# A Mamba loop issued in the order of its text, with two head phases per step and decays four steps ahead

## The chip, the cores and the metric

One core of one Trainium2 chip runs the kernel. The time is the device time of one launch in microseconds (us). The kernel before takes 10208.33 us (median of 4 runs, 10189.17 to 10220.28). "PEclk" or "granted clock" is the share of full speed that the clock throttle let TensorE have. In the listings PE is TensorE, DVE is VectorE, ACT is ScalarE and POOL is GpSimd. L654 is line 654 of that kernel's file, so one operation has different line numbers in different kernels.

## The reference, cut to what matters

The whole is an attention block, a Mamba layer along the image, a two-way Mamba along rows and then along columns, and a small filter. The change touches only the Mamba parts:

```python
# one Mamba: x [channel 128, time], state 16 per channel
xc = silu(conv4(x) + b);  z = gate projection of the same input
dt, B, C = split(x_proj(xc));  dt = softplus(dt_proj(dt) + dt_b)
h  = exp(dt * A) * h + dt * B * xc          # for every state: the scan
y  = (sum over states of h * C) + xc * D
out = out_proj(y * silu(z))
```

## The kernel before

The sequence is cut into units of 768 columns. There are 120: 24 in layer 1 and two passes of 48 in layer 2 (rows, then columns). A unit has a head (convolution, gate, Silu, softplus, B, C), 16 steps (a decay `da`, an input `u_s`, a scan, a product with C), four pairs of gathers, and a tail. Heads are generators: each `yield` is a place where the loop does a step of the recurrence first.

```python
def head(self, u):
    raw = self.work("raw", 2 * CH)                  # two buffers
    for j in range(2):
        p = self.convolved(u, u.c0 + j * HALF)      # four products, one PSUM tile "m"
        yield
        nc.scalar.activation(u.xc[:, halves[j]], p, AF.Identity, bias=w.conv_b)
    ...                                             # two gate products, copied to raw
    self.k.tc.keep_in_program_order(nc.scalar.activation(raw, raw, AF.Silu))
    self.table = nc.scalar.preload_act_table_set("natural_log_exp_and_others")
    ...
    for j in range(2):
        p = self.mm(w.step, u.xc[:, halves[j]])     # dt_proj, a half at a time, tile "m"
        yield
        nc.scalar.activation(e[:, halves[j]], p, AF.Abs, bias=w.dt_b)
        nc.scalar.activation(u.dt[:, halves[j]], p, AF.Relu, bias=w.dt_b)
    nc.scalar.activation(e, e, AF.Exp, scale=-1.0)
    nc.scalar.activation(log, e, AF.Ln, bias=1.0)
    ...
    nc.vector.tensor_scalar(kept, e, 1.0, 1.0, ALU.add, ALU.subtract)
    ...                                             # GpSimd: e, log, dt, u, memset of dt

def gather(self, u, step):                          # y_ssm: four small products
    ...
    if q == 3:                                      # twice per unit
        nc.vector.scalar_tensor_tensor(yv, u.xc[:, cols], u.w.Dp, u.py[:, :HALF], ALU.mult, ALU.add)
        nc.gpsimd.tensor_mul(u.y[:, cols], yv, u.gate[:, cols])

def run(self, units):
    ...
    for n, (u, s) in enumerate(steps):
        if s == 1:
            other = chain(self.head(units[i + 1]), units[i - 1].tail(units[i - 1]))   # shortened
        if s == self.STEPS - 2:
            for _ in other:
                pass
        self.spread(at(n + 1), at(n + 2))           # u_s of the next step, dt_s of the one after
        self.scan(u, s)                             # VectorE: multiply u_s by B, scan
        next(other, None)
        if s % 2 == 0 and n >= 2:
            self.gather(*steps[n - 1])
```

The order in which each engine gets these instructions is not the order of this text: a scheduler of the framework arranges them. In PSUM, `dt_s` has one buffer, `u_s` two, the gather one, and all other products share the one buffer "m". The trace has two records for each product of the text, so the four products of a gather are its x8.

## Time and profile before

| before (profiled run, span 10211.9 us) | value |
|---|---|
| granted clock, whole span | 0.858 |
| VectorE busy | 7503.5 us (73%) |
| TensorE busy | 8743.6 us (86%) |
| layer 1, from one unit's `kept` to the next | 59.5 us |
| layer 2, the same, first and last pass | 56.6 and 55.9 us |

The number after the second bar of a group is idle time of the engine right before these instructions, and the arrow names what ended it. Three more groups of the kernel before, from the view of groups with different shapes kept apart, are needed later. They are VectorE's other operations that depend on TensorE or ScalarE:

```profile
L676 DVE SCALAR_TENSOR_TENSOR yv<-raw,cols,y_ssm 128x384 f32<-128x384 f32 x240 | 141.4, 589 | 10.3 <-PE y_ssm L665 10.3
L578 DVE TENSOR_SCALAR kept<-e 128x768 f32<-128x768 f32 x120 | 82.9, 691 | 81.5 <-ACT e L569 81.4
L869 DVE SCALAR_TENSOR_TENSOR xa<-lin,cols,xa 64x384 f32<-64x384 f32 x96 | 75.6, 788 | 58.9 <-PE lin L867 58.9
```

The reader is to see that all three are small: before the change, VectorE's idle time in the Mamba part is the 1146 us ahead of the multiply, some 0.1 us ahead of each scan, and little else.

### The profile page before, as it was taken

What the parts mean: (1) busy time and instruction counts of PE and PEld (TensorE: products, weight loads), DVE (VectorE), ACT (ScalarE), POOL (GpSimd) and SP (SyncE); (2) the same over time, 40 slices, a digit from 0 to 9 for tenths busy, and PEclk for the clock granted to TensorE, in tenths of its full rate; (3) what the DMA queues carried; (4) which work ended last, traced back from release to release, by engine and by line L of the source; (5) the groups of instructions that cost most, each with busy time, mean ns of one, the idle gap of its engine ahead of it and who ended that gap; (6) DMA issues with size and microseconds to landing.
All of it is one profiled execution on the core that took longest, in us unless ns stands there. A gap on an engine that the chain in (4) does not pass through costs nothing.

```text
span 10211.9 us, 100390 instructions
## 1 busy us (share of the span) xinstructions
PE 8743.6 (86%) x38998; PEld 2948.9 (29%) x38998; DVE 7503.5 (73%) x6112; ACT 4291.8 (42%) x5082; POOL 4701.9 (46%) x3186
## 2 busy tenths in 40 slices
PE   9999999999868888868888888888688888888884
PEld 3333333333222222222222222222222222222221
DVE  4666646666658777767787777777778777787778
ACT  3444434444334334434444444444344444444442
POOL 0000000000036666636666666666367666676663
PEclk9999989999977777768888888888688888898887
DMA  0000000000000000000000000000000000000000
GB/s 24 1 1 1 1 1 1 1 1 1 1 0 1 1 1 1 1 0 1 1 1 1 1 1 1 1 1 1 0 1 1 1 1 1 1 1 1 1 1 19
DMA packets 2220, 17.25 MB, mean 2 GB/s; under 512 B 196, under 2 KB 324, under 8 KB 1096
## 3 DMA queue, kind: packets, MB, share of 16 engines
q1 hardware_dynamic: 1440, 9.44, 0.2%
q8 instruction: 307, 5.03, 0.2%
q14 instruction: 177, 1.45, 0.0%
q10 hardware_dynamic: 296, 1.33, 0.0%
HBM read 6.05 MB, written 4.72 MB: 1 GB/s over the span
## 4 chain that ended last, share of the span: by engine, by line
PE 27%; DVE 24%; POOL 15%; issue 5%; ACT 2%; DVEq 0%; POOLq 0%; ACTq 0%
DVE h L652 13%; PE u_s L622 7%; POOL hc L654 7%; DVE u_s L642 7%; PE y_ssm L665 6%; PE conv L536 4%; PE mm L513 4%; POOL e L579 2%; POOL log L580 2%; POOL dt L584 2%; PE dt_s L622 1%; PE conv L530 1%; DVE h L648 1%; POOL yg L677 1%; PE lin L863 1%
## 5 line engine op out<-in xcount | busy, mean ns | idle before, releaser
L654 POOL TENSOR_TENSOR hc<-h,C 128x768 f32<-128x768 f32 x1920 | 3484.0, 1819 | 1746.0 <-DVE h L652 1551.5
L652 DVE TENSOR_TENSOR_SCAN h<-da,u_s 128x768 f32<-128x768 f32 x1536 | 2693.8, 1754 | 199.5 <-DVE u_s L642 4.8
L633 ACT ACTIVATE da<-dt_s 128x768 f32<-128x768 f32 x1920 | 1554.2, 809 | 2936.6 <-PE dt_s L622 2914.2
L642 DVE TENSOR_TENSOR u_s<-u_s,B 128x768 f32<-128x768 f32 x1920 | 1825.6, 951 | 1146.0 <-PE dt_s L622 1059.0
L622 PE MATMUL u_s<-u,spread 32*128 32x384 f32 x7680 | 2221.5, 629 | 429.3 <-DVE h L652 325.5
L622 PE MATMUL dt_s<-dt,decay 32*128 32x384 f32 x7680 | 2119.3, 630 | 8.7 <-ACT da L633 3.5
L267 DVE TENSOR_TENSOR acc_e<-acc_e,e 128x1536 f32<-128x1536 f32 x792 | 1390.0, 1755 | 763.4 <-ACT e L211 724.7
L665 PE MATMUL y_ssm<-hc,gather 128*32 128x384 f32 x7680 | 1433.9, 598 | 457.9 <-POOL hc L654 456.6
L211 ACT ACTIVATE e<-f_exp 128x1536 f32<-128x1536 f32 x864 | 1207.0, 1449 | 1218.4 <-PE f_exp L201 1218.4
L622 PEld LDWEIGHTS u_s<-u,spread 32*128 32x128 f32 x7680 | 775.5, 217 | 1871.8 <-DVE h L652 805.9
L240 POOL TENSOR_TENSOR xa<-xa,t_att 64x512 f32<-64x512 f32 x36 | 45.3, 1259 | 2725.1 <-ACT t_att L238 2725.1
L218 PE MATMUL y_att<-e,xb 128*64 128x512 f32 x5184 | 1242.5, 601 | 0.0
L201 PE MATMUL f_exp<-theta,phi 64*128 64x512 f32 x5184 | 1235.7, 608 | 0.6 <-ACT e L211 0.6
L536 PE MATMUL conv<-xb,taps 64*128 64x384 f32 (+3 forms) x1536 | 694.2, 604 | 118.2 <-ACT raw L550 117.5
L648 DVE TENSOR_TENSOR_SCAN h<-da,state,u_s 128x384 f32<-128x384 f32 x768 | 737.4, 1000 | 48.4 <-DVE u_s L642 1.0
L622 PEld LDWEIGHTS dt_s<-dt,decay 32*128 32x128 f32 x7680 | 692.4, 217 | 186.7 <-ACT da L633 126.7
L201 PEld LDWEIGHTS f_exp<-theta,phi 64*128 64x128 f32 x5184 | 468.8, 187 | 756.7 <-issue 463.4
L665 PEld LDWEIGHTS y_ssm<-hc,gather 128*32 128x32 f32 x7680 | 232.0, 116 | 1429.7 <-POOL hc L654 854.4
L218 PEld LDWEIGHTS y_att<-e,xb 128*64 128x64 f32 x5184 | 341.3, 136 | 830.7 <-issue 830.1
L513 PE MATMUL mm<-raw,bc 128*128 128x384 f32 x960 | 519.2, 627 | 27.7 <-ACT dt L568 23.0
L550 ACT ACTIVATE raw<-conv,cols 128x384 f32<-128x384 f32 x240 | 139.6, 582 | 909.6 <-PE conv L536 415.1
L536 PEld LDWEIGHTS conv<-xb,taps 64*128 64x128 f32 x1536 | 332.7, 227 | 457.1 <-ACT raw L550 180.4
(147 smaller groups left out, 6005.7 us busy)
## 6 DMA issues: line engine op xcount, KB each, us to landing
xa<-in_x SPq DMA_DIRECT2D x6, 768.0 KB, 10.1
out<-xb SPq DMA_DIRECT2D x4, 1152.0 KB, 4.4
mats<-in_mats ACTq DMA_DIRECT2D x1, 1218.0 KB, 7.8
cols<-in_cols ACTq DMA_DIRECT2D x1, 71.5 KB, 9.5
dtw<-in_dtw ACTq DMA_DIRECT2D x1, 10.0 KB
```

The source lines that it names most:

```text
L201: nc.tensor.matmul(fs[j // 3][:, bass.ts(j % 3, NB)], lhsT=phi[at, bass.ts(m // 2, P)], rhs=theta[at, bass.ts(i, NB)], start=True, stop=True,)
L211: nc.scalar.activation(e, f, AF.Exp)
L218: nc.tensor.matmul(y[rows_of(m % 2)], lhsT=g[:, m, :], rhs=es[j // 3][:, bass.ts(j % 3, NB)], start=m < 2, stop=m >= KEYS - 2,)
L267: nc.vector.tensor_add(acc, acc, e)
L513: self.nc.tensor.matmul(p[:, :HALF], lhsT=lhsT, rhs=rhs, start=True, stop=True)
L536: self.nc.tensor.matmul(p3[:, :, o], lhsT=lhsT, rhs=x3[:, :, i], **flags)
L622: self.nc.tensor.matmul(self.side((u.pu if what == 0 else u.pda)[step], j), lhsT=(self.t.spread if what == 0 else u.w.decay)[rows, q], rhs ...
L633: self.nc.scalar.activation(da, u.pda[step][:, NB - HALF : NB + HALF], AF.Exp)
L642: nc.vector.tensor_mul(two(bx), two(bx), each(u.B))
L652: nc.vector.tensor_tensor_scan(h[:, way], da[:, way], bx[:, way], 0.0, ALU.mult, ALU.add)
L654: nc.gpsimd.tensor_mul(two(hc), two(h), each(u.C))
L665: nc.tensor.matmul(u.py[32 * r : 32 * r + 32, :HALF], lhsT=self.t.gather[:, q], rhs=u.hc[s][:, j * HALF : (j + 1) * HALF], start=q == 0, s ...
```

## The change

The intent is to take the order of the Mamba loop out of the scheduler's hands and write it down. The `with tc.manual_schedule()` block issues instructions as the text has them. The head of the next unit starts one whole unit ahead (`LEAD = 16`) and moves by two phases per step: one between the spreads and the exp of a decay, one behind that exp. Decays run four steps ahead (`AHEAD = 4`) in six buffers, `raw` has three, `hc` (the product with C) six in place of five, and the gathers come two steps later. `dt_p`, the step product, is now one 768-wide tile in the single buffer of `dt_s`, so that Abs and Relu are one instruction each.

```diff
-        raw = self.work("raw", 2 * CH)
+        raw = self.work("raw", 2 * CH, bufs=3)
...
-        for j in range(2):
-            p = self.mm(w.step, u.xc[:, halves[j]])
-            yield
-            nc.scalar.activation(e[:, halves[j]], p, AF.Abs, bias=w.dt_b)
-            nc.scalar.activation(u.dt[:, halves[j]], p, AF.Relu, bias=w.dt_b)
+        p = self.ps_da.tile([P, 2 * NB], FP, tag="p", name="dt_p")
+        for j in range(2):
+            nc.tensor.matmul(self.side(p, j), lhsT=w.step, rhs=u.xc[:, halves[j]], start=True, stop=True)
+        v = p[:, NB - HALF : NB + HALF]
...
+        nc.scalar.activation(e, v, AF.Abs, bias=w.dt_b)
+        nc.scalar.activation(u.dt, v, AF.Relu, bias=w.dt_b)
+        yield
...                          # more yields: about two per step of the recurrence
-            self.spread(at(n + 1), at(n + 2))
+            self.inputs(at(n + 1))
+            later = at(n + self.AHEAD)
+            p = self.decays(later)
+            next(head, None)
+            next(tail, None)
+            self.decay(later, p)
+            if s == self.STEPS - self.LEAD and i + 1 < len(units):
+                head = self.head(units[i + 1])
+            if s == self.STEPS - 2 and i:
+                tail = units[i - 1].tail(units[i - 1])
+            next(head, None)
+            next(tail, None)
             self.scan(u, s)
-            next(other, None)
-            if s % 2 == 0 and n >= 2:
-                self.gather(*steps[n - 1])
+            if s % 2 == 0 and n >= 4:
+                self.gather(*steps[n - 3])
...
-        m.run(units)
+        with tc.manual_schedule():
+            m.run(units)
```

## The prediction

> **What bounds the kernel now.** I read the page's 40 slices first, then the costliest groups, then the timeline of single units in the second half. The slices show two regimes: until slice 11 the attention, which the diff does not touch, and from about 2940 us the five Mamba passes.
>
> ```profile
> PE   9999999999868888868888888888688888888884
> ...
> DVE  4666646666658777767787777777778777787778
> ...
> PEclk9999989999977777768888888888688888898887
> ```
>
> In the Mamba part no engine is full: TensorE reads 8, VectorE 7 to 8. The groups say what VectorE waits for:
>
> ```profile
> L654 POOL TENSOR_TENSOR hc<-h,C 128x768 f32<-128x768 f32 x1920 | 3484.0, 1819 | 1746.0 <-DVE h L652 1551.5
> L652 DVE TENSOR_TENSOR_SCAN h<-da,u_s 128x768 f32<-128x768 f32 x1536 | 2693.8, 1754 | 199.5 <-DVE u_s L642 4.8
> L633 ACT ACTIVATE da<-dt_s 128x768 f32<-128x768 f32 x1920 | 1554.2, 809 | 2936.6 <-PE dt_s L622 2914.2
> L642 DVE TENSOR_TENSOR u_s<-u_s,B 128x768 f32<-128x768 f32 x1920 | 1825.6, 951 | 1146.0 <-PE dt_s L622 1059.0
> ```
>
> A step is one multiply and one scan on VectorE, 1.07 + 1.67 = 2.74 us from start to start. A layer-2 unit has 16 steps (43.84), the `kept` operation (0.45), two `yv` (1.0) and its share of the tail (0.85): 46.1 us of VectorE. The timeline has 48 such units from 4547.69 to 7271.57, so 56.7 us each: 10.6 us of holes. Layer 1 (step 2.90, 49.0 us of work) takes 1431.5/24 = 59.6 us, also 10.6 us of holes. The 1146 us of idle time before the multiply, over 120 units, is nearly all of it. The timeline shows two big holes per unit. The first, where one unit follows another:
>
> ```profile
> 6014.47 1.75 DVE L652 TENSOR_TENSOR_SCAN h<-da,u_s 128x768 f32<-128x768 f32 x1
> ...
> 6017.39 1.81 POOL L586 TENSOR_TENSOR u<-dt,raw 128x768 f32<-128x768 f32 x1
> ...
> 6019.49 0.97 DVE L642 TENSOR_TENSOR u_s<-u_s,B 128x768 f32<-128x768 f32 x1 [3.26 <-PE dt_s L622]
> ```
>
> The head's GpSimd chain (e, log, dt, u) ends too late, and the new unit's spreads wait for it. The second, four to six steps later:
>
> ```profile
> 6037.97 1.00 POOL L677 TENSOR_TENSOR yg<-yv,raw 128x384 f32<-128x384 f32 x1
> 6039.00 0.58 ACT L550 ACTIVATE raw<-conv,cols 128x384 f32<-128x384 f32 x1 [3.80 <-POOL yg L677]
> ...
> 6039.63 4.43 PE L536 MATMUL conv<-xb,taps 64*128 64x384 f32 x8 [1.75 <-ACT raw L550]
> ...
> 6047.14 0.97 DVE L642 TENSOR_TENSOR u_s<-u_s,B 128x768 f32<-128x768 f32 x1 [5.08 <-PE dt_s L622]
> ```
>
> ScalarE may not write the next `raw` until GpSimd has used the old gate (two buffers); TensorE waits, then runs the second convolution in 4.43 us, where the first, at 6034.23, took 2.80.
>
> **What the Trainium skill says.** "TensorE: Matmul & The Clock Gate", Part 1, has the clock halve after an idle window of about 3.4 us and return after a busy one. The trace agrees: between 4600 and 7200 us I sorted TensorE's gaps by the rate of the first products after them. Of gaps under 1.25 us 1 of 125 led to half rate, of 1.25 to 2.25 us 49 of 98, of 3.25 to 3.75 us 37 of 37. "ScalarE: Activation LUTs", section "What ACT_TABLE_LOAD costs", gives about 1283 ns a load; the trace has two of 1.28 around each Silu:
>
> ```profile
> 6050.40 1.28 ACT L556 ACT_TABLE_LOAD   x1
> 6051.70 1.48 ACT L556 ACTIVATE raw<-raw 128x1536 f32<-128x1536 f32 x1
> ...
> 6053.20 1.28 ACT L557 ACT_TABLE_LOAD   x1
> ...
> 6054.49 0.81 ACT L633 ACTIVATE da<-dt_s 128x768 f32<-128x768 f32 x1
> ```
>
> so 4.09 us in which ScalarE does no exp. "PSUM — Partial Sum Buffer", section "Engine vs sequencer instructions", says that ScalarE, VectorE and GpSimd queues are strict FIFO and matmuls start in program order. That decides this change: before, the order was a scheduler's; afterwards it is the text's, and an instruction that waits holds back everything behind it.
>
> **The change, part by part.** Work is nearly unchanged: one 768-wide Abs and Relu replace two 384-wide each, and decays lead by four steps instead of two. What it removes: with three `raw` buffers and the head from step 0 on, the second hole's cause is gone (5 us); with u and dt ready at step 12, so is the first hole's (3 us). Both were worth about 8 of the 10.6.
>
> What it adds I get by walking one layer-2 unit in text order. Durations from the timeline: the four spreads of a step run together in 0.93 us (half rate 1.65); spread to exp 1.02; product 0.84 to the next, convolution half 2.73 (half rate 4.36), gather 0.78 (half rate 1.44). T(n) is the start of multiply n; the spreads of step n start at T(n)+0.14, because u_s(n+1) needs scan n−1's buffer, so 1.6 us of TensorE delay is free.
> - Steps 0 to 2, two convolutions in front of u_s(2) and u_s(3): the third multiply comes 0.95 us late. Where a real tail lies there (every second unit) its `lin` products (about 3 us each) stall VectorE 2.4 us instead. Mean 1.7.
> - Step 4, Silu: exp(8) ends at T4+2.3 (TensorE is 0.35 late there), loads and Silu until T6+0.9, exp(9) T6+1.7. `dt_p` shares the single dt_s buffer, so it starts only then: 1.7 us of product, Abs and Relu 1.75, dt_s(10) 0.95, exp(10) 0.85, Exp of e 0.85: T6+7.8. `kept` stands in VectorE's queue in front of multiply 7, which was due at T6+2.74. Loss 5.1. TensorE idles over 3 us ahead of `dt_p`, so mostly the clock halves: 1.6 to 2 us more.
> - Step 12: the memset of dt stands on GpSimd behind hc(10), dt, hc(11) and u, so it ends at T13+1.9. dt_s(16) waits for it in TensorE's queue, then the gather, then u_s(14): multiply 14 is 1.95 late, and since TensorE idled 3.6 us, at half rate 3.8. Layer 1 has no memset and loses nothing here.
>
> Layer 2 at full clock: 1.7 + 5.1 + 1.95 = 8.75, thus 54.9 us per unit; with the half rate about 12.5, thus 58.6. Layer 1: 0.5 + 4.4 + 0.3 gives 54.2, with the half rate 56.4. Against 56.7 and 59.6:
> - full clock: 96 × (−1.8) + 24 × (−5.4) = −303 us, 9910;
> - half rate in each such gap: 96 × 1.9 + 24 × (−3.2) = +106 us, 10320.
> The first decays, now four one after another, cost three passes about 3 us each, 10 in all.
>
> **The rivals.** (a) VectorE becomes the bound: text order with four decays in hand hides everything; units take 46 to 48 us and the time is about 9100 to 9300. For it: VectorE steps already run at 2.74 without gaps for ten steps on end, and the constants look tuned. Against it: `kept` and the shared `dt_p` buffer in the walk above. (b) The new waits only replace the old ones: the sum with the half rate, 10300. For it: 37 of 37 long gaps halve the clock. Against: a stall also gives the other engines time to catch up, and I may have put a phase wrong by one step. (c) TensorE becomes the bound: 16 × 0.93 + 8 × 0.78 + 5.5 + 8 × 0.84 + 3 = 36 us per unit at full clock, far under 46; only a clock at half throughout would do it, some 65 us and 11000. The granted 0.85 speaks against that.
>
> **Range and chances.** The walk spans 9910 to 10320, with its middle near 10120; I take 10110, a little under, since a change of this kind is usually made to win and my error in reading an order is more likely to have invented a stall than to have missed a hole. Range 9650 to 10430. Faster by over 2% means under 10008: 0.39. Within 2%: 0.43. Slower: 0.18.
>
> **What would show it.** In the changed profile the idle time before L642's multiply because of dt_s should fall from 1059 to under 400 us; the idle time before `kept` should rise from under 60 us to 300 to 700, ended by ACT e; ScalarE's Abs should wait on `dt_p`; a wait of dt_s for the memset should appear on TensorE in layer 2 only; the 3.8 us ScalarE wait on yg should be gone. Layer 1 should gain more per unit than layer 2. If `kept` shows no idle time, the walk is wrong and rival (a) holds. If the mean matmul stays at 600 ns or more, the half rate is as I feared.

## The result and the profile after

The changed kernel takes 10840.35 us (median of 4, 10818.72 to 10861.24) against 10208.33 us. The ratio is 1.0621, with a 95% interval from 1.0593 to 1.0649: slower by 6.2%. Ratios here are the mean time of one kernel's fast runs over that of the other's of the same rounds, so they differ a little from the ratio of the medians. The predicted 10110 us and the range up to 10430 were wrong.

The slices of the changed kernel's page, 40 over a span of 10859.5 us:

```profile
PE   9999999999587787677777777777777777777874
...
PEclk9999989999778777577877787776677777777776
```

Against before, most of TensorE's 8s are now 7s, and in the second half the granted clock is mostly 7, in places 6, where it was mostly 8. The view of windows shows the last pass (48 units), first of the kernel before, then of the changed one. The columns are the window, then its length, the busy time of PE, PEld (weight loads), DVE, ACT and POOL with the number of instructions, the granted clock, and the DMA share and rate.

```profile
7408.00:10096.00 2688.00, 2272.95 (x10994) 758.33 (x10992) 2133.68 (x1725) 1151.93 (x1566) 1823.56 (x1098) 0.85 0.00 1
```

```profile
7674.00:10743.00 3069.00, 2402.70 (x10972) 808.54 (x10968) 2126.91 (x1724) 1146.48 (x1470) 1814.82 (x1098) 0.73 0.00 1
```

VectorE does the same work (2134 and 2127 us) in 381 us more. So the loss is idle time of VectorE, not work. Measured from one `kept` to the next, a layer-2 unit takes 62.7 us in the first pass and 64.0 in the last (before 56.6 and 55.9). A layer-1 unit takes 57.9 (before 59.5): layer 1 did gain.

VectorE's groups of the changed kernel, shapes kept apart, show where the idle time is (`kept` now lies in the buffer of `u`, hence its name `u<-e`):

```profile
L664 DVE TENSOR_TENSOR_SCAN h<-da,u_s 128x768 f32<-128x768 f32 x1536 | 2693.8, 1754 | 197.0 <-DVE u_s L654 5.3 <-POOL yg L689 1.0 <-ACT da L646 1.0
L654 DVE TENSOR_TENSOR u_s<-u_s,B 128x768 f32<-128x768 f32 x1920 | 1820.2, 948 | 635.3 <-PE dt_s L629 581.2 <-PE u_s L629 50.9
L688 DVE SCALAR_TENSOR_TENSOR yv<-raw,cols,y_ssm 128x384 f32<-128x384 f32 x240 | 144.3, 601 | 340.1 <-PE y_ssm L677 340.1
L896 DVE SCALAR_TENSOR_TENSOR xa<-lin,cols,xa 64x384 f32<-64x384 f32 x96 | 75.8, 790 | 120.1 <-PE lin L894 120.1
L584 DVE TENSOR_SCALAR u<-e 128x768 f32<-128x768 f32 x120 | 67.2, 560 | 842.7 <-ACT e L578 842.7
```

The multiply lost 511 us of idle time, as intended. `kept` gained 761, `yv` 330, the tail's `lin` 61. The balance is +641 us, and the spans differ by 648: the account closes.

Two groups of TensorE name what it waits for:

```profile
L629 PE MATMUL dt_s<-dt,decay 32*128 32x384 f32 x7680 | 2264.5, 673 | 398.3 <-POOL dt L608 332.1 <-ACT dt L571 37.3 <-ACT da L646 21.7
L565 PE MATMUL dt_p<-raw,step 128*128 128x384 f32 x480 | 346.0, 876 | 336.6 <-ACT da L646 326.5
```

The decays of the next unit wait 332 us for the memset of dt (L608), and `dt_p` waits 327 us for an exp of ScalarE, because it shares the single buffer of `dt_s`. The same in time, from the timeline of one layer-2 unit (start, length, engine, instruction, and in brackets the engine's idle time before it):

```profile
5995.75 0.81 ACT L646 ACTIVATE da<-dt_s 128x768 f32<-128x768 f32 x1
5996.61 2.36 PE L565 MATMUL dt_p<-raw,step 128*128 128x384 f32 x4 [2.58 <-ACT da L646]
...
5999.87 0.89 ACT L571 ACTIVATE dt<-dt_p,cols 128x768 f32<-128x768 f32 x1
6000.81 1.65 PE L629 MATMUL dt_s<-dt,decay 32*128 32x384 f32 x4 [0.26 <-ACT dt L571]
...
6004.08 0.56 DVE L584 TENSOR_SCALAR u<-e 128x768 f32<-128x768 f32 x1 [6.19 <-ACT e L578]
...
6018.84 1.65 PE L629 MATMUL u_s<-u,spread 32*128 32x384 f32 x4 [2.34 <-DVE h L664]
...
6023.77 0.11 POOL L608 MEMSET dt<- 128x8 f32 x1
...
6023.94 1.65 PE L629 MATMUL dt_s<-dt,decay 32*128 32x384 f32 x4 [3.45 <-POOL dt L608]
6025.52 1.51 PE L677 MATMUL y_ssm<-hc,gather 128*32 128x384 f32 x8
...
6028.66 0.97 DVE L654 TENSOR_TENSOR u_s<-u_s,B 128x768 f32<-128x768 f32 x1 [4.39 <-PE dt_s L629]
```

The first hole: a table load and Silu hold up an exp, that exp holds the buffer that `dt_p` needs, the exp of `e` comes after Abs, Relu and one more decay, and `kept` stands in VectorE's queue for it, 6.19 us, ahead of a multiply whose inputs were there. The second: dt_s for the next unit waits 3.45 us for the memset, and then the gather and the next u_s still stand in front of the multiply. The four records of one `dt_s` take 0.91 us at full clock (from 6035.22 on in this unit) and 1.65 here: TensorE ran at half rate behind both gaps. The memset's gap did not bring that on, though. The `u_s` before it already takes 1.65 us, behind a pause of 2.34 us in which TensorE was only ahead of VectorE's scan; and the record of the granted clock that lies in the trace was already at half rate at the start of 91 of the 94 waits of over 2 us for the memset (57 of 117 for `dt_p`).

By adding up the stretches of TensorE's timeline in which known groups run at the longer of their two durations, I get the share of time at half rate between 4600 and 7200 us: 0.34 before, in stretches of 4.2 us on average, and 0.45 after, in stretches of 12.1 us. This measure is worked out from the trace and is rough. The trace's own clock record, added up in the same window, has 0.30 before, in stretches of 7.8 us on average, and 0.47 after, in stretches of 12.5 us (the view of windows has granted clocks of 0.85 and 0.77). So the shares hold within 0.05, here and for the runs below, but the stretches grew by a factor of 1.6 and not of three. The expectations quoted below use it too, some of them over other windows.

### The profile page after: what moved, and what is told of

Same layout as the page of the kernel before. It is cut to its first block, busy times and chain, and to the rows that moved or that the text cites. A ratio compares the mean times of both kernels' runs of the same rounds, so it can differ in the third digit from the quotient of the medians.

```text
span 10859.5 us, 100467 instructions
## 1 busy us (share of the span) xinstructions
PE 8841.2 (81%) x38998; PEld 2997.5 (28%) x38998; DVE 7487.6 (69%) x6112; ACT 4276.4 (39%) x4842; POOL 4681.1 (43%) x3186
## 4 chain that ended last, share of the span: by engine, by line
PE 32%; DVE 16%; POOL 11%; ACT 9%; issue 6%; DVEq 0%; POOLq 0%; ACTq 0%
PE u_s L629 7%; POOL hc L666 7%; PE conv L538 6%; DVE h L664 6%; PE dt_s L629 5%; PE y_ssm L677 4%; DVE u_s L654 4%; PE dt_p L565 3%; DVE h L660 2%; ACT da L646 2%; PE mm L515 2%; ACT raw L559 2%; POOL u L604 2%; ACT L559 1%; ACT L560 1%
## 5 line engine op out<-in xcount | busy, mean ns | idle before, releaser
L629 PE MATMUL dt_s<-dt,decay 32*128 32x384 f32 x7680 | 2264.5, 673 | 398.3 <-POOL dt L608 332.1
L629 PEld LDWEIGHTS u_s<-u,spread 32*128 32x128 f32 x7680 | 745.6, 233 | 2444.5 <-DVE h L664 1216.3
L677 PE MATMUL y_ssm<-hc,gather 128*32 128x384 f32 x7680 | 1077.5, 641 | 5.2 <-POOL hc L666 5.2
L629 PEld LDWEIGHTS dt_s<-dt,decay 32*128 32x128 f32 x7680 | 717.1, 228 | 752.1 <-POOL dt L608 440.0
L584 DVE TENSOR_SCALAR u<-e 128x768 f32<-128x768 f32 x120 | 67.2, 560 | 842.7 <-ACT e L578 842.7
L565 PE MATMUL dt_p<-raw,step 128*128 128x384 f32 x480 | 346.0, 876 | 336.6 <-ACT da L646 326.5
L585 POOL TENSOR_TENSOR e<-e,u 128x768 f32<-128x768 f32 x120 | 217.0, 1808 | 931.0 <-ACT log L579 931.0
L515 PE MATMUL mm<-raw,bc 128*128 128x384 f32 x960 | 547.0, 658 | 20.3 <-ACT B L582 16.9
```

Source lines behind the costliest of these rows:

```text
L629: self.nc.tensor.matmul(self.side(p, j), lhsT=lhsT[rows, q], rhs=rhs[rows, cols], start=True, stop=True)
L677: nc.tensor.matmul(u.py[32 * r : 32 * r + 32, :HALF], lhsT=self.t.gather[:, q], rhs=u.hc[s][:, j * HALF : (j + 1) * HALF], start=q == 0, s ...
```

## The experiments

Fifteen kernels gave a result, and all were correct; the label e8 has no run on record. The kernel before: medians 10196.46 for the first four, 10192.49 for the next four, 10216.08 for the next three, 10233.07 for the twelfth, 10199.02 for the last three.

| run | built on | edit | median us | ratio to before [95%] |
|---|---|---|---|---|
| e1_kept_late | after | `kept` two steps later | 11226.32 | 1.0996 [1.0968, 1.1025] |
| e2_yv_late | after | `yv` two steps later | 10771.64 | 1.0549 [1.0519, 1.0578] |
| e3_u_early | after | u and memset earlier | 10919.66 | 1.0710 [1.0684, 1.0736] |
| e4_scheduler | after | scheduler's order | 10709.05 | 1.0507 [1.0486, 1.0529] |
| e7_warm | after | unread products in two gaps | 10716.59 | 1.0497 [1.0454, 1.0540] |
| e9_dt_halves | after | `dt_p` in halves again | 10466.62 | 1.0276 [1.0237, 1.0316] |
| e5_before_text | before | text order | 11857.57 | 1.1626 [1.1589, 1.1662] |
| e6_before_raw3 | before | three `raw` buffers | 9722.34 | 0.9539 [0.9510, 0.9568] |
| e10_halves_sched | after | halves, scheduler's order | 9962.32 | 0.9770 [0.9734, 0.9807] |
| e11_raw3_two | before | three `raw`, two phases | 10636.07 | 1.0413 [1.0386, 1.0440] |
| e12_text20 | after | text order, all named waits mended | 10347.62 | 1.0133 [1.0106, 1.0159] |
| e13_text20_warm | e12 | unread product, buffer "m" | 11376.86 | 1.1088 [1.1049, 1.1127] |
| e14_warm_free | e12 | unread product, buffer of `u_s` | 10558.06 (one run slow) | 1.0296 [1.0219, 1.0374] |
| e15_split_conv | e12 | convolutions in two pieces | 10166.30 | 0.9973 [0.9913, 1.0033] |
| e16_split_warm | e12 | e14 and e15 together | 10352.38 | 1.0149 [1.0127, 1.0170] |

**One hole at a time.** The first question was whether the largest hole, `kept`'s, is the loss.

```diff
 # e1_kept_late, head of the changed kernel
-        nc.vector.tensor_scalar(kept, e, 1.0, 1.0, ALU.add, ALU.subtract)
-        nc.gpsimd.tensor_sub(e, e, kept)
         ...                                         # two steps of B and C products
+        nc.vector.tensor_scalar(kept, e, 1.0, 1.0, ALU.add, ALU.subtract)
+        nc.gpsimd.tensor_sub(e, e, kept)
         nc.gpsimd.tensor_add(log, log, e)
```

> Edit: the kept operation (VectorE) and the subtraction behind it (GpSimd) move from step 7 to step 9, nothing else. Theory Q (the loss is made of single instructions that wait in an in-order queue in front of ready work): VectorE's idle time before kept falls from 843 us to under 150; the GpSimd chain to u and the memset ends about 2 us later, so the wait of dt_s for the memset grows by about 2 us in each of the 96 layer-2 units. Sum: 10840 - 700 + 190, thus 10270 to 10450 us. Rival R (the chain Silu, dt_p, exp, Ln is simply too long and its time comes back in another wait, whatever instruction stands in front): 10740 us or more.

The hole went (843 to 75 us) and the kernel became 386 us slower. VectorE's multiply waits instead:

```profile
L654 DVE TENSOR_TENSOR u_s<-u_s,B 128x768 f32<-128x768 f32 x1920 | 1826.3, 951 | 1606.4 <-PE dt_s L629 1182.1 <-PE u_s L629 421.1
```

The multiply's idle time rose by 971 us, `yv`'s from 340 to 426, TensorE's wait for the memset from 332 to 483. TensorE was late in any case, and the wait of VectorE had hidden that. Its own timeline in this run shows a second thing:

```profile
6003.33 1.65 PE L629 MATMUL u_s<-u,spread 32*128 32x384 f32 x4 [2.34 <-DVE h L664]
6009.90 1.65 PE L629 MATMUL dt_s<-dt,decay 32*128 32x384 f32 x4 [4.92 <-POOL dt L608]
...
6022.76 5.41 PE L538 MATMUL conv<-xb,taps 64*128 64x384 f32 x8
...
6031.13 5.41 PE L538 MATMUL conv<-xb,taps 64*128 64x384 f32 x8
...
6042.66 1.01 PE L515 MATMUL mm<-xb,mats 64*128 64x384 f32 x2
```

After the 4.92 us gap the half rate lasts from 6009.90 to about 6043, some 33 us. It had begun before the gap: the first line shown already runs at it, and the trace's clock record has half rate from 6001.9 to 6042.9. From 6009.90 on, lines left out included, no product of TensorE has idle time ahead of it. Both convolutions take 5.41 us instead of 2.80.

The next two runs move one other waiter each.

```diff
 # e2_yv_late: yv and yg leave gather() and are issued two steps later
-            yv = self.work("yv", HALF)
-            nc.vector.scalar_tensor_tensor(yv, u.xc[:, cols], u.w.Dp, u.py[:, :HALF], ALU.mult, ALU.add)
-            nc.gpsimd.tensor_mul(u.y[:, cols], yv, u.gate[:, cols])
+            u.half = cols
...
+            if s % 8 == 4 and n >= 12:
+                self.out(steps[n - 5][0])           # the same two instructions
```

> Edit: yv (VectorE) and yg (GpSimd) are issued two steps after the gather they read, nothing else. Theory Q: VectorE's idle time before yv falls from 340 us to under 40 and the time by 200 to 300 us, to 10540 to 10640. Rival R (TensorE is late behind the two convolutions at steps 0 to 2, so the multiply waits for u_s instead): the idle time before the multiply grows from 635 us by about as much, and the time stays above 10740.

`yv`'s idle time fell from 340 to 17 us, but the multiply's rose from 635 to 804 and the tail's from 120 to 236. Of 323 us that went, some 70 were won (medians).

```diff
 # e3_u_early: behind the add of dt, two yields fewer before u and the memset
         nc.gpsimd.tensor_add(u.dt, u.dt, log)
-        yield
-        yield
         nc.gpsimd.tensor_mul(u.u, u.dt, u.xc)
```

> Edit: u and the memset of dt come directly behind the addition to dt (step 11), by taking out two yields. Theory Q: the memset ends about 1.8 us earlier and TensorE's gap in front of dt_s(16) shrinks from 3.6 to about 1.9 us, so that only about half of the following products run at half rate; the layer-2 hole of 4.4 us falls to 1 to 2 us: 240 to 330 us less, 10510 to 10600; layer 1, which has no memset, is unchanged within 10 us. Rival R: hc(11) now stands behind u and the memset and the scan waits for its buffer instead; time above 10740.

TensorE's wait for the memset fell from 332 to 182 us and the multiply's idle time from 635 to 539, while `yv` rose to 398 and the tail to 202. The kernel was 79 us slower. So a named hole is not a cost: in all three runs most or more of its idle time came back elsewhere.

**The order and the shared buffer.** Four runs cross the two parts of the change that the walk had blamed.

```diff
 # e4_scheduler: both places
-        with tc.manual_schedule():
-            m.run(units)
+        m.run(units)
```

> Edit: the two manual-schedule blocks are taken out, so that the scheduler orders the instructions again; buffers, phases and the lead of four stay. Theory Q: the scheduler moves kept, yv and the gathers behind ready work, idle time before kept under 100 us, before yv under 40; time 9800 to 10300 us. Rival P (the parts themselves are at fault: dt_p in the single dt_s buffer, the convolutions in whole, the lead of four): 10600 us or more also under the scheduler.

The waits of `kept` (79 us) and `yv` (9 us) are gone, as they belong to text order, but the time falls by 131 us only:

```profile
L654 DVE TENSOR_TENSOR u_s<-u_s,B 128x768 f32<-128x768 f32 x1920 | 1826.7, 951 | 1679.2 <-PE u_s L629 1225.6 <-PE dt_s L629 452.5
```

```profile
L629 PE MATMUL dt_s<-dt,decay 32*128 32x384 f32 x7680 | 2139.5, 636 | 470.5 <-ACT da L646 466.9 <-POOL dt L601 3.6
```

TensorE's dt_s wait 467 us for an exp of ScalarE in this run, that is, for their single buffer (22 us in the changed kernel, where `dt_p` waits 327 in their stead). The buffer that `dt_p` shares is in the way in either order; e10_halves_sched below is the same kernel without the sharing (and with the small shifts of e9_dt_halves, next), its dt_s wait 39 us for an exp, and it is 747 us faster.

```diff
 # e9_dt_halves: the changed kernel's step product in two halves through "m", as before
-        p = self.ps_da.tile([P, 2 * NB], FP, tag="p", name="dt_p")
-        ...                                         # two products, Abs and Relu of 768
+        for j in range(2):
+            p = self.mm(w.step, u.xc[:, halves[j]])
+            yield
+            nc.scalar.activation(e[:, halves[j]], p, AF.Abs, bias=w.dt_b)
+            nc.scalar.activation(u.dt[:, halves[j]], p, AF.Relu, bias=w.dt_b)
+            if not j:
+                yield
```

Exp and Ln come one step later in it, and two later yields are dropped to keep the head's length. These shifts were not tried apart from the halves.

> Edit: dt_p is undone: the step product goes through the small buffer in two halves as in the kernel before, each with its own Abs and Relu; Exp and Ln one step later, two yields fewer behind. Theory D (the shared dt_s buffer is what stops TensorE, so that u_s stands behind dt_s(10) behind Relu): waits of TensorE for dt_p and of dt_s for Relu (over 350 us) go, kept's idle time falls from 843 us to under 200, time 9900 to 10300 us. Rival (Silu's 4 us on ScalarE with the lead of four is itself the stop): kept's time moves to the multiply, 10600 us or more.

This is the largest gain of any single edit in text order: 374 us.

```profile
L582 DVE TENSOR_SCALAR u<-e 128x768 f32<-128x768 f32 x120 | 113.7, 948 | 339.2 <-ACT e L576 339.2
```

`kept`'s idle time fell from 843 to 339 us, and this time nothing else rose by as much: the multiply has 660, `yv` 271, the tail 205. The other factor alone, text order with the parts of before:

```diff
 # e5_before_text: the kernel before, its three ordering hints removed
-            with self.k.tc.issue_after(self.table.ins):
-                self.nc.scalar.activation(da, u.pda[step][:, NB - HALF : NB + HALF], AF.Exp)
+            self.nc.scalar.activation(da, u.pda[step][:, NB - HALF : NB + HALF], AF.Exp)
...
-        m.run(units)
+        with tc.manual_schedule():
+            m.run(units)
```

> Edit, on the kernel before: text order alone (its Mamba loops in a manual-schedule block, the three ordering hints taken out since they are not allowed there); phases, buffers and the lead of two stay. Theory T (text order as such costs): well over the kernel before, 10700 us or more. Theory P (the rebuilt parts are at fault): within 3% of the kernel before, 9900 to 10500 us. My estimate is in between: the text of before has one phase per step and Silu with a lead of only two, so that the scan should wait for exp 3 us per unit more, 10500 us.

Text order alone costs 16%. The parts rebuilt for it in the change therefore win back some 1000 us (11858 to 10840), but they start from a loss of 1650.

```diff
 # e10_halves_sched: e9's edit, and no manual_schedule
-        with tc.manual_schedule():
-            m.run(units)
+        m.run(units)
```

> Edit, on the changed kernel: the step product in halves again (as in e9) and the scheduler's order (as in e4), so that of the change only the three raw buffers, the two phases, the lead of four and the deeper da and hc buffers stay. Theory S (two causes that add up: text order in place of the scheduler's, and dt_p in the dt_s buffer; the rest of the change is good or neutral): near the kernel before with three raw buffers (9722 us), 9600 to 9850 us; the multiply's wait for u_s falls from 1226 us (e4) to under 150. Rival (the lead of four, with the decay product in front of the next inputs in TensorE's queue, costs by itself): 10000 us or more.

It takes 9962 us and misses its range, but beats the kernel before by 2.3% (its interval lies on both sides of 2%, so by the threshold of 2% its verdict is "unclear"). `kept` waits 116 us, `yv` 11, the multiply 760. With `dt_p` shared, leaving text order is worth 131 us (10840 to 10709); with halves it is worth 504 (10467 to 9962). Undoing both wins 878 us, undoing one alone 131 and 374: each cause hides part of what the other costs.

**What the third `raw` buffer is worth, and two phases.** Both on the kernel before.

```diff
 # e6_before_raw3 (and e11_raw3_two)
-        raw = self.work("raw", 2 * CH)
+        raw = self.work("raw", 2 * CH, bufs=3)
 # e11_raw3_two only, in run()
             next(other, None)
+            next(other, None)
```

> Edit, on the kernel before: three raw buffers in place of two, nothing else (the part of the change that I had expected to win). If the hole of 5 us at the second convolution is made by the wait for the gate, ScalarE's wait on yg (368 us in all) goes and the time falls by 300 to 550 us, to 9650 to 9900 us. Rival: the scheduler uses the freedom to start the head earlier and the hole only moves; 10050 us or more.

```profile
L642 DVE TENSOR_TENSOR u_s<-u_s,B 128x768 f32<-128x768 f32 x1920 | 1824.6, 950 | 626.9 <-PE dt_s L622 580.3 <-PE u_s L622 44.9
```

The multiply's idle time falls from 1146 to 627 us and the clock rises from 0.858 to 0.898. This one word makes the fastest kernel, 9722.34 us, 4.6% less time than before and some 10% less than the change. The change's two phases per step add nothing to it:

> Edit, on the kernel before: three raw buffers (as e6) and two pieces of the head per step in place of one, so that the head's text, and with it the scheduler's priority, ends about six steps earlier. If the hole of 3 us between units comes from the head's GpSimd chain ending late, the idle time before the multiply falls from 627 us to under 350: 9350 to 9600 us. Rival (the scheduler takes priority from readiness and the chain stays where it was): 9680 to 9800 us.

Two pieces of head per step cost some 900 us against one (10636 and 9722). The tail's `lin` now waits 456 us, the multiply 841. Both expectations missed it.

**The clock.** TensorE's half rate could be the cause or only follow from the waits.

```diff
 # e7_warm: unread products ahead of the two long waits
         yield
+        for j in range(2):
+            self.mm(w.step, u.xc[:, halves[j]])     # before dt_p
...
+            if s == self.STEPS - self.AHEAD and later is not None:
+                for j in range(3):
+                    self.mm(u.w.step, u.xc[:, :HALF])   # before the decays behind the memset
```

> Edit: products whose result nobody reads are issued where TensorE would idle: two of the step product (128 rows, 384 columns) in front of dt_p, three in front of dt_s(16). The traces of the first four runs show a thing I had not reckoned with: half-rate stretches of TensorE last 14 us on average after the change (4 us before), up to 41 us[...]. Theory C (clock: the two gaps of over 3 us start stretches of half rate, in which TensorE is the bound): the share of time at half rate falls from 0.51 to under 0.38, granted clock of the last pass from 0.73 to over 0.80, time 10100 to 10500 us although there is more work. Theory Q (waits in queues alone, the clock follows): time 10750 us or more.

The granted clock rose from 0.799 to 0.863, which is above that of the kernel before, and the share of half rate fell from 0.45 to 0.27. The time fell by 124 us only. `kept` still waits 5.6 us per layer-2 unit. So a clock like the one of before doesn't bring the time of before back. This run alone can't say how much the unread work took of what the clock gave. e4_scheduler adds no work and agrees: its granted clock is 0.851, near the 0.858 of before, and it is 5.1% slower.

**What is left of text order.** Can text order be mended?

```diff
 # e12_text20: e9's halves, and the order mended by hand
-    LEAD = 16
+    LEAD = 20
...
 # kept two steps after Ln; log, dt, u and the memset spread over more phases but ending earlier;
 # yv two steps after its gather (e2); the tail at step 8
+            ahead, phase = divmod(n + self.LEAD, self.STEPS)
+            if (phase == 0 or n == 0) and ahead < len(units):
+                head = self.head(units[ahead])
+            if s == 8 and i:
                 tail = units[i - 1].tail(units[i - 1])
```

> Edit, on the changed kernel, still in text order, all waits that I found mended at once: the head starts at step 12 of the unit before (LEAD 20), the step product in halves, kept at step 5, two steps behind the Exp that it reads, u and the memset done a step before the dt_s that needs them, yv two steps behind its gather, the tail at step 8. Theory Q (text order costs what single waits in queues cost, and these can be placed away): kept, yv and memset waits all under 60 us, idle time before the multiply under 400 us, 9300 to 9700 us. Rival (text order costs more than single placements can mend, since the order must suit both clock rates): 9900 us or more.

The waits that the prediction had walked through are gone: `kept` 77 us, memset 21, `yv` 97. The multiply has 1127. It gains 493 us on the changed kernel and is still 1.3% slower than before. Its timeline shows what took their place:

```profile
6042.93 5.41 PE L538 MATMUL conv<-xb,taps 64*128 64x384 f32 x8
...
6051.40 0.97 DVE L655 TENSOR_TENSOR u_s<-u_s,B 128x768 f32<-128x768 f32 x1 [5.23 <-PE dt_s L630]
```

A convolution at half rate stands in TensorE's queue ahead of the next spreads. The last four runs ask whether the rate or the block is to be blamed.

```diff
 # e13_text20_warm: in run(), each step
+            self.nc.tensor.matmul(self.ps_m.tile([P, NB], FP, tag="m", name="warm")[:, : HALF // 2],
+                                  lhsT=u.w.step, rhs=u.xc[:, : HALF // 2], start=True, stop=True)
             self.inputs(at(n + 1))
```

> e12_text20 (10347.62 us, 0.77 granted clock in the last pass, TensorE at half rate for a share of 0.46, multiply idle 1127 us) with one unread full-row product of 192 columns ahead of the spreads of every step. It costs TensorE 0.42 us a step at full clock (1920 of them, some 810 us spread over the Mamba part, beside other work). Theory C (what is left of text order is the half rate: a convolution of 5.41 us instead of 2.80 stands in front of u_s): full-row products bring the clock back[...], so the half-rate share falls under 0.3, the multiply's idle time under 700 us, and the time is 9800 to 10100 us. Theory O (what is left is the order itself: two convolutions ahead of u_s, whatever their rate): the clock rises but the multiply keeps over 900 us and the time stays within 10250 to 10500 us. If the half-rate share does not fall, full-row products do not bring the clock back and neither is tested.

This was a bad experiment: the unread product needs buffer "m" and waits 814 us for its readers, at the head of TensorE's queue. It became 1029 us slower and tells nothing of the clock. It was done again without that wait:

```diff
 # e14_warm_free: in spread(), for u_s only; the spread overwrites it
         p = pool.tile([P, 2 * NB], FP, tag="p", name=name)
+        if warm is not None:
+            self.nc.tensor.matmul(self.side(p, 0)[:, : HALF // 2], lhsT=warm.w.step,
+                                  rhs=warm.xc[:, : HALF // 2], start=True, stop=True)
```

> e12_text20 (10347.62 us; between 4600 and 7200 us TensorE at half rate for a share of 0.43, multiply idle 1127 us) with an unread full-row product of 192 columns written into u_s's own buffer right before each spread overwrites it, so that unlike in e13_text20_warm (11377 us, the product waited 814 us for readers of the shared product buffer) it waits for nothing new. Theory C (what is left of text order is the half rate): the half-rate share falls under 0.3, the multiply's idle time under 800 us, time 9900 to 10150 us in spite of 0.42 us more work a step. Theory O (what is left is the queue: two convolutions ahead of u_s at any rate, or any more work in front of u_s): the multiply keeps over 1000 us and the time is 10350 to 10700 us.

The share of half rate fell from 0.43 to 0.36 only, short of what the test needed. The multiply's idle time rose to 1400 us and the time by some 200 (medians of the fast runs). It fits the second theory (any more work in front of `u_s` costs), but it is no clean refutation of the first.

```diff
 # e15_split_conv: in convolved(), behind the second of four taps
+                if j == 1:
+                    yield
...
-            p = self.convolved(u, u.c0 + j * HALF)
+            p = yield from self.convolved(u, u.c0 + j * HALF)
...
-        yield
-        yield
         nc.gpsimd.tensor_mul(u.u, u.dt, u.xc)
```

> e12_text20 with each convolution half issued in two pieces of two taps, in two phases, so that at most 2.7 us of half-rate convolution stand in front of a u_s, in place of 5.41. Theory O (the block in the queue is the cause, and its size counts): 4 of the some 9.4 us of multiply holes per unit go, multiply idle from 1127 to under 750 us, time 9850 to 10100 us, with the half-rate share little changed (over 0.35). Theory C (the clock is the cause): splitting changes neither the clock nor the work, the holes are only spread over more steps, multiply idle over 950 us and time 10250 to 10450 us.

It is some 180 us faster than e12_text20 with a half-rate share of 0.46, not lower; over the whole span its clock was a little higher in some runs, but its two runs at a granted clock of 0.818 took 10208 and 10215 us, where e12_text20's run at 0.818 took 10319. So the size of the block matters without a better clock. But the multiply keeps 1025 us, where the theory of the block wanted under 750, and the time lies between the two ranges. The kernel only draws level with before:

```profile
L657 DVE TENSOR_TENSOR u_s<-u_s,B 128x768 f32<-128x768 f32 x1920 | 1825.0, 951 | 1025.5 <-PE dt_s L632 972.4 <-PE u_s L632 51.5
```

Nearly all of it is still a wait for the spreads in TensorE's queue.

> Both edits of e14_warm_free and e15_split_conv in one kernel. If both causes act, it is the fastest of the three, 9700 to 9950 us, and the first one of the text-order kernels to beat the kernel before by more than 2%; if only one acts it equals the better of the two within 80 us; if the unread work costs more than the clock gives, it is slower than e15_split_conv.

Here the half-rate share did fall, to 0.27 from e15's 0.46, and the kernel was slower than e15_split_conv by 186 us. So the unread work costs more than the clock gives, which was the third case of the expectation.

## Why the prediction was wrong

**The bound was read rightly.** VectorE's work per unit did not change, and the whole difference is its idle time (641 of 648 us).

**The places of the holes were right, nearly all.** Counting multiplies after `kept` in the changed trace, layer-2 units have holes of 6.6 us (first pass) and 6.9 (last) at `kept`, in front of multiply 7; of 4.3 and 4.2 at multiply 14; and of 1.1 and 1.8 at the third multiply of the next unit. The walk named these three. It gave 5.1 to 7.1, 1.95 to 3.8, and 0.95 us. Of the signs that it asked for, five came: `kept` waits for ACT e (842.7 us, above the 300 to 700 named); Abs waits for `dt_p`, 355 us in all; dt_s waits for the memset, 332.1 us, so 3.5 us for each of 96 layer-2 units against 3.6 worked out; the ScalarE wait on yg (368 us in all before) is gone; and layer 1 gained while layer 2 lost. The mean spread is 673 ns, over the 600 named for the half rate, but it was 629 before, so that sign could hardly fail. The other sign failed: the multiply's idle time because of dt_s fell from 1059 to 581, not under 400.

**The step that failed first is "Steps 0 to 2, two convolutions in front of u_s(2) and u_s(3)", put at "Mean 1.7".** The walk followed the spreads behind the convolutions and forgot that the gather stands behind them too, and that `yv` waits for the gather at the head of VectorE's queue. That hole is 2.5 us per unit in the first pass and 3.6 in the last. With the tail (1.3 and 1.0) and the third multiply, this term measures 4.9 and 6.4 us in place of 1.7. In e2_yv_late the wait is gone and only 70 us of the time went with it, so it is not the cause of the whole.

**The second step is the middle between "full clock" and "half rate in each such gap".** Products behind both long gaps ran at half rate, so the sum with it, 10320, was the one to take; the middle and then "a little under" gave away 210 us of the miss of 730. At these two holes that sum had about the right size (6.6 to 6.9 us at `kept` against up to 7.1, 4.2 to 4.3 at multiply 14 against 3.8). At the second this was luck: its reason, "since TensorE idled 3.6 us", is not what halved the clock, which had fallen before the memset's gap (91 of 94).

**The rest of the miss.** Holes per layer-2 unit, over 0.3 us each kind, add up to 15.8 us (first pass) and 17.5 (last), where the worst case had 12.5. That is 3.3 and 5.0 us for 48 units each, 400 us of the remaining 520, and nearly all of it lies in the term of the first step (3.2 and 4.7 us more than 1.7). It is not shown that the long half rate made this term so large: e7_warm had less of it and still has 357 us at `yv`, against 340. Layer 1 at 57.9 instead of 56.4 adds some 37. The last 80 or so I have not traced.

**The rivals.** (a), VectorE as the bound, is refuted by 842.7 us at `kept`. (b), new waits in place of old, is what happened, at more than the 10300 it was given. (c), TensorE's clock, was dismissed because "the granted 0.85 speaks against that". The grant is no constant of the kernel, it fell to 0.73 in the last pass. Yet giving it back in e7_warm won 124 of the 632 us. Whether a higher clock got without extra work would win more was not tried.

**The chances.** "A change of this kind is usually made to win" was no evidence, and it moved the number the wrong way.

What is shown: text order and the shared `dt_p` buffer together make the loss, as far as e9_dt_halves takes out the sharing alone. Without both (e10_halves_sched) the kernel is 2.3% faster than before; without the shared buffer alone it is 2.8% slower (e9_dt_halves), without text order alone 5.1% (e4_scheduler). What stays open: why e10_halves_sched is 240 us slower than e6_before_raw3, which has neither the long lead nor the two phases (e11_raw3_two says that two phases alone can cost more than this, but by another wait); and what the rest of text order is made of, since e15_split_conv still has 1025 us ahead of its multiply.

## What to carry to other kernels

Idle time listed ahead of an instruction is not what removing its wait will win: in strict queues the next late producer shows up at once, so try the removal before believing the sum. When an order is written by hand, follow every queue, also the small products behind a long block, and do the walk at the slower clock, since blocks behind a pause can run longer, even behind one in which TensorE was only ahead. Before rebuilding a loop, try its cheapest part alone: one more `raw` buffer won 4.6%, and the rebuilt loop around it lost 6.2%.

## What the Trainium skill lacked or had wrong

- "TensorE: Matmul & The Clock Gate", Part 1, has the clock halve after at least one idle window of about 3.4 us and return after at least one busy one. The clock records of all 17 kept traces, cut into such windows (between 4600 and 7200 us every stretch is a multiple of 3.413 us), show what counted. Of 675 full-rate windows in which TensorE was busy for under 0.4 of the time, all were followed by half rate; with over 0.8 busy, 19 of 4352. So shorter pauses than 3.4 us suffice. Of half-rate windows with TensorE busy for over 0.98, full rate followed 44 of 817 where the products filled on average under half of the 128 rows, and 501 of 606 where they filled over three quarters. This goes with the 33 us of half rate without a pause in e1_kept_late, mostly 32-row spreads and 64-row convolutions; it is a sorting of traces and no experiment.
- The same page, "Terms", puts the penalty of the slow clock at the throttled time, times the share of pulses lost. As an estimate by that rule, granted clocks of 0.799 and 0.863 over their spans differ by some 700 us; e7_warm won 124, with unread products as extra work. The rule doesn't say what the clock is worth where TensorE is not what the kernel waits for: a share of half rate of 0.27 instead of 0.46 came with 186 us more (e16_split_warm beside e15_split_conv).
- "ScalarE: Activation LUTs", "What ACT_TABLE_LOAD costs", adds about 1380 ns of drain to each load. No such time shows here: load, Silu and load start at 5991.66, 5992.95 and 5994.46 in the changed kernel, and the next exp at 5995.75, so 4.09 us for two loads of 1.28 and a Silu of 1.48.
- No page weighs an order written by hand against a scheduler's. Here the same kernel, but for three ordering hints, took 11858 us in text order and 10192 in the scheduler's (e5_before_text).
